# Issue order of every engine from a list schedule that the kernel makes over its own trace

## The chip, the cores and the metric

The kernel runs on one core of a Trainium2 chip. The core has five engines with instruction queues of their own: TensorE (PE, matmuls, with its weight loads as PEld), VectorE (DVE), ScalarE (ACT), GpSimd (POOL) and SyncE (SP, which only issues transfers). The metric is the device time of one execution in microseconds. The kernel before took 3448.2 us (median of three executions, 3447.78 to 3453.78).

## The reference

A decoder of four layers in float32, on x of 8 batches x 256 tokens x 256 features, with a context of 8 x 77 tokens. Every sublayer is followed by a residual and a layer normalisation:

```python
x = _layernorm(x + _L0_attn_ref(x, ...), axis=-1)           # causal, 16 heads, 8-bit fake quantisation
x = _layernorm(x + _L0_xattn_ref(x, ctx_1024, ...), axis=-1)  # 16 heads of 64
x = _layernorm(x + _L0_ffn_ref(x, ...), axis=-1)            # 8 experts, 2 per token, gelu
x = _layernorm(x + _L1_attn_ref(x, ...), axis=-1)           # causal softmax attention
x = _layernorm(x + _L1_xattn_ref(x, ctx_1024, ctx_1024, mask, ...), axis=-1)
x = _layernorm(x + _L1_ffn_ref(x, ...), axis=-1)            # 8 experts with a capacity, and a shared one, silu
x = _layernorm(x + _L2_attn_ref(x, ...), axis=-1)           # linear attention, elu features
x = _layernorm(x + _L2_xattn_ref(x, ctx_1024, ...), axis=-1)  # normalised heads, rope on q
x = _layernorm(x + _L2_ffn_ref(x, ...), axis=-1)            # 14 experts, 2 per token, and 2 shared ones
x = _layernorm(x + _L3_attn_ref(x, ...), axis=-1)           # state space layer: conv, chunked scan
x = _layernorm(x + _L3_xattn_ref(x, ctx_1024, ...), axis=-1)  # linear attention
x = _layernorm(x + _L3_ffn_ref(x, ...), axis=-1)            # butterfly up, exact gelu, butterfly down
```

The quantisation of layer 0 scales by maxima over all tokens, so it needs every batch before it can go on. The routed feed-forwards need the routing of all tokens before the first expert tile.

## The kernel before, in words

The class `Build` holds the program. Tokens lie in 16 tiles `x` of 128 x 256 and, transposed, in four tiles `xt`. The attention sublayers loop over the 8 batches of 256 tokens; each batch goes through a few hand-offs from PE to DVE, ACT and POOL and back. Helpers spread the work: `later` and `tick` keep generators of unfinished work, and a loop takes a step of them where the author placed a call, so that the end of one batch is traced between pieces of the next. `side` and `fill` do the same for weights and shared experts. The source's order is therefore already interleaved by hand.

All matmuls go through `mm` (line 164), which writes a PSUM tile of 512 float32 columns from `ps()`. These tiles share one tag, `ps`, in a pool of eight buffers, one for each bank. Most other tiles have a tag with one to five buffers.

The routed feed-forwards (`routed_tiles`, lines 1121 to 1133) run a fixed number of tiles (`U0`, `U2` = 19, 22), then a conditional block for more. POOL fetches each tile's weights and rows by indirect transfers (lines 1068 and 1093), DVE copies the result out (line 1166) and SP stores it. The next sublayer collects the results: `collected` gathers rows on POOL (line 1093) and adds them on DVE (line 2796), once per tile and choice.

The program's order on each engine is not written out. A scheduler of the language takes the traced instructions and decides the issue order of every engine and the buffer of every tile, in keeping with data dependencies. Where its order was not wanted, the author tied instructions with `after` (line 1039): the adds of line 2796 wait for the previous add and for marks set in the running loop (`gate`, `gates`, `mark`); the weight maximum of line 352 waits for the input maximum of line 477; the copy of line 1864 waits for the routing of the batch before (`routed`); the butterfly weights of lines 2505 and 2524 wait for the last expert tile (`tile_end`).

In layer 3, one loop over batches does the state space layer, the cross-attention and the feed-forward. Its activations use several function tables: silu (L2176), exp (L2211, L2433), exact gelu (L2361), for instance:

```python
for n in range(2):
    nc.scalar.activation(E[n], E[n], AF.Exp, scale=-1.0)
```

## Time and profile before

The profiled execution took 3453.26 us, of which the span from first to last instruction is 3451.5 us, with a mean granted clock of 0.908. By stages, in microseconds (PE and DVE are busy times; the clock is the granted share of TensorE's full clock):

| Stage from:to | Length | PE | DVE | Clock | What runs |
|---|---|---|---|---|---|
| 0:86.3 | 86.3 | 41.08 | 63.26 | 0.68 | loads, quantisation of layer 0 |
| 86.3:431.4 | 345.1 | 256.29 | 264.11 | 0.73 | layer 0 attention |
| 431.4:517.7 | 86.3 | 67.23 | 46.48 | 0.79 | its projection, cross-attention begins |
| 517.7:776.6 | 258.9 | 245.15 | 156.37 | 0.95 | layer 0 cross-attention, routing |
| 776.6:1035.4 | 258.8 | 258.80 | 28.09 | 1.00 | layer 0 experts |
| 1035.4:1121.7 | 86.3 | 76.20 | 43.13 | 0.88 | collecting, layer 1 attention begins |
| 1121.7:1294.3 | 172.6 | 170.79 | 108.58 | 1.00 | layer 1 attention |
| 1294.3:1380.6 | 86.3 | 73.88 | 53.64 | 0.92 | layer 1 cross-attention begins |
| 1380.6:1553.2 | 172.6 | 164.33 | 139.79 | 1.00 | layer 1 cross-attention |
| 1553.2:1639.5 | 86.3 | 76.72 | 44.86 | 0.80 | routing |
| 1639.5:2157.2 | 517.7 | 513.38 | 108.18 | 1.00 | layer 1 experts |
| 2157.2:2416.0 | 258.8 | 226.54 | 169.04 | 0.97 | layer 2 attention |
| 2416.0:2674.9 | 258.9 | 206.79 | 166.79 | 0.77 | layer 2 cross-attention |
| 2674.9:2847.5 | 172.6 | 172.02 | 74.08 | 1.00 | layer 2 experts |
| 2847.5:2933.8 | 86.3 | 78.57 | 33.51 | 0.93 | collecting |
| 2933.8:3365.2 | 431.4 | 367.72 | 301.78 | 0.89 | layer 3 |
| 3365.2:3451.5 | 86.3 | 63.24 | 26.65 | 0.90 | last batches of layer 3 |

An engine that waits for nothing in a stage bounds it. PE's busy time counts a matmul until its modelled end, so a high share is not yet full work; [...]busy time times clock says how much full-clock work was done.

### The profile page before, as it was taken

The page shows a single profiled execution, that of the slowest core. Times are in us where ns is not written, and L with a number is a line of the kernel's source. Part 1 is how long each engine was busy: PE and PEld are TensorE (multiplying, and loading weights), DVE is VectorE, ACT ScalarE, POOL GpSimd, SP SyncE. Part 2 cuts the span into 40 slices and gives each one's busy share as a digit, 9 for nine tenths or more (in the row PEclk, how much of TensorE's full clock was granted, in tenths as well). Part 3 has the DMA queues.
Part 4 walks back from the last instruction along what each step waited for, and adds up shares of the span by engine and source line. Part 5 has one row for each costly group of instructions (what it writes and reads, how often), then busy time and mean ns, then how long its engine had stood idle before and what let it go on. Part 6 is the DMA issues. An engine that isn't in the chain of part 4 may idle for free. (4 is left out here: it accounts for less than half of the span.)

```text
span 3451.5 us, 49595 instructions
## 1 busy us (share of the span) xinstructions
PE 3058.7 (89%) x19199; PEld 2186.5 (63%) x19210; DVE 1828.4 (53%) x4835; ACT 1082.8 (31%) x2426; POOL 932.6 (27%) x1379
## 2 busy tenths in 40 slices
PE   4787679989998998998999999998787999888887
PEld 3444357768886776665555777565555786567766
DVE  7887556641005666785111221576675443687763
ACT  4666422222222333332111111344222112244332
POOL 2222323343312211232000000331333563433331
PEclk6777779989998999998999999999787999889998
DMA  9900110025532000001010343100002562000000
GB/s 337 333 1 2 37 44 13 19 82 197 183 134 86 19 30 14 20 14 59 14 37 12 117 139 114 42 20 8 7 20 68 193 216 90 25 7 4 7 7 10
DMA packets 132658, 239.96 MB, mean 70 GB/s; under 512 B 14585, under 2 KB 104449, under 8 KB 124737
## 3 DMA queue, kind: packets, MB, share of 16 engines
q1 hardware_dynamic: 108160, 136.71, 11.9%
q0 software_dynamic: 23104, 98.95, 8.4%
q8 instruction: 156, 2.56, 0.3%
q10 hardware_dynamic: 1152, 1.05, 0.1%
q14 instruction: 86, 0.70, 0.1%
HBM read 156.98 MB, written 79.69 MB: 69 GB/s over the span
## 5 line engine op out<-in xcount | busy, mean ns | idle before, releaser
L164 PE MATMUL ps<-xt,w 128*128 128x256 f32 (+1 forms) x1408 | 446.4, 466 | 8.7 <-issue 8.7
L164 PE MATMUL ps<-w,hT 128*128 128x256 f32 (+1 forms) x1792 | 397.4, 379 | 0.0
L164 PEld LDWEIGHTS ps<-w,hT 128*128 128x128 f32 (+1 forms) x1792 | 329.9, 186 | 56.5 <-issue 6.0
L164 PE MATMUL ps<-gT,w 128*128 128x256 f32 (+1 forms) x1472 | 356.9, 400 | 5.7 <-ACT gT L152 3.0
L164 PEld LDWEIGHTS ps<-xt,w 128*128 128x128 f32 x1408 | 264.8, 195 | 151.2 <-issue 129.8
L164 PEld LDWEIGHTS ps<-gT,w 128*128 128x128 f32 x1472 | 276.2, 191 | 76.6 <-ACT gT L152 3.9
L164 PE MATMUL ps<-w,oT 128*128 128x256 f32 x704 | 165.0, 390 | 1.1 <-ACT oT L152 0.2
L164 PEld LDWEIGHTS ps<-w,oT 128*128 128x128 f32 x704 | 135.6, 195 | 34.0 <-issue 11.1
L1155 ACT ACTIVATE hT<-ps,more 128x256 f32<-128x256 f32 x152 | 72.0, 474 | 199.0 <-PE ps L164 199.0
L1166 DVE COPY y<-ps 128x512 f32<-128x512 f32 x41 | 28.3, 690 | 174.8 <-PE ps L164 174.8
L1232 DVE TENSOR_TENSOR hT<-hT,ps 128x512 f32<-128x512 f32 x56 | 38.5, 688 | 149.9 <-PE ps L164 149.5
L694 ACT ACTIVATE e<-ps,nm 128x128 bf16<-128x128 f32 (+1 forms) x256 | 103.9, 458 | 39.9 <-DVE nm L689 23.9
L244 PE MATMUL ps<-ident,x 128*128 128x128 f32 x288 | 57.3, 311 | 61.8 <-DVE x L272 46.9
L272 DVE TENSOR_SCALAR x<-res,mv,rs 128x256 f32<-128x256 f32 x112 | 51.4, 459 | 111.6 <-POOL rs L192 111.6
L284 POOL TENSOR_TENSOR xb<-x,rows 128x256 f32<-128x256 f32 x80 | 61.4, 773 | 178.0 <-DVE res L289 174.1
L1228 ACT ACTIVATE hT<-ps 128x512 f32<-128x512 f32 x56 | 33.4, 597 | 237.7 <-PE ps L164 237.7
L1723 POOL TENSOR_TENSOR kpad<-kpad,rows 128x256 f32<-128x256 f32 (+1 forms) x10 | 7.3, 730 | 363.5 <-DVE hu L1672 276.2
L911 POOL TENSOR_TENSOR P<-P,z 128x1232 f32<-128x1232 f32 (+1 forms) x32 | 55.2, 1736 | 169.6 <-DVE z L910 169.6
L978 PE MATMUL ps<-PT,V 77*64 77x256 f32 x512 | 95.0, 429 | 6.6 <-ACT PT L152 4.4
L1587 ACT ACTIVATE f<-ps,neg 128x512 f32<-128x512 f32 x128 | 77.4, 689 | 57.2 <-PE ps L1584 57.2
L963 PEld LDWEIGHTS ps<-ident,P 128*77 128x77 f32 x512 | 60.1, 155 | 51.7 <-issue 23.9
L1588 DVE SCALAR_TENSOR_TENSOR f<-ps,f 128x512 f32<-128x512 f32 x128 | 79.0, 680 | 25.8 <-ACT f L1587 25.8
(670 smaller groups left out, 6436.1 us busy)
## 6 DMA issues: line engine op xcount, KB each, us to landing
l2x<-zero SPq DMA_DIRECT2D x28, 1024.0 KB, 11.2
l0x<-zero SPq DMA_DIRECT2D x16, 1024.0 KB, 10.8
w<-in_L_ffn_rg SPq DMA_DIRECT2D x8, 1024.0 KB, 7.0
w<-in_L_ffn_ru SPq DMA_DIRECT2D x8, 1024.0 KB, 5.0
w<-in_L_ffn_rd SPq DMA_DIRECT2D x8, 1024.0 KB, 5.6
l2e<-y SPq DMA_DIRECT2D x22, 256.0 KB, 2.3
l0e<-y SPq DMA_DIRECT2D x19, 256.0 KB, 2.5
w<-in_L_xattn_Wk SPq DMA_DIRECT2D x4, 1024.0 KB, 5.0
```

Of the source, the lines that this page charges most:

```text
L164: self.nc.tensor.matmul(out, lhsT, rhs, start=(i == 0), stop=(i == last))
L244: self.nc.tensor.transpose(ps[:, k * P : (k + 1) * P], x[:, k * P : (k + 1) * P], self.ident)
L272: nc.vector.tensor_scalar(t, r, mv[:, 0:1], rs, ALU.subtract, ALU.mult)
L284: self.nc.gpsimd.tensor_tensor(t, self.X[i], row, ALU.add)
L694: nc.scalar.activation(e[:, : (t + 1) * P], ps[j][:, i, :], AF.Exp, bias=nm[:, t, h : h + 1], accum_out=z[:, t, h : h + 1],)
L911: eng.tensor_tensor(pr, pr, z.unsqueeze(2).to_broadcast([P, n, SC]), ALU.mult)
L963: nc.tensor.transpose(psv[:, m, t * P : (t + 1) * P], Pt[t][:, 2 * n + m, :], self.ident)
L978: nc.tensor.matmul(po[64 * m : 64 * m + 64, :S], V[:, h * 64 : (h + 1) * 64], ahead[n % 2][:, m, :], start=True, stop=True,)
L1155: nc.scalar.activation(hT[:, f + m, :], ps[:, m * 256 : (m + 1) * 256], func, bias=more[:, f + m : f + m + 1])
L1232: nc.vector.tensor_tensor(hT[:, f, :], hT[:, f, :], ps, ALU.mult)
L1587: nc.scalar.activation(f[:, j], ps[j], AF.Exp, bias=neg1)
L1588: self.mark = nc.vector.scalar_tensor_tensor(f[:, j], ps[j], 1.0, f[:, j], ALU.max, ALU.min)
```

## The change

The kernel is now traced twice. The first trace ends in a new class `Arrange`, which reads the traced instructions, works out their dependencies and durations, and makes a list schedule: for each engine it looks at up to 30 ready instructions not more than 300 places past the oldest unfinished one, and takes the first in source order that can start within `SLACK` of the earliest. It places PSUM tiles in banks as it goes. The second trace puts each PSUM tile under the tag of its bank, and ties every instruction to the one before it on its engine, so that the language's scheduler has no choice left. The ties that the author had made by hand are taken out; those that guard rows in memory (`scattered`, `zeroed`) stay.

```diff
+class Arrange:
+    ENGINES = ("PE", "DVE", "Activation", "Pool", "SP")
+    SIGNAL = {("DVE", "Pool"): 77, ("Activation", "Pool"): 69, ("PE", "Pool"): 100, ("DVE", "PE"): 44, ("Activation", "PE"): 43, ("Pool", "Pool"): 77}
+    TABLES = [{f, "Identity", "Copy", "Square", "Relu", "Abs"} for f in ("Exp", "Ln", "Silu", "Gelu", "Gelu_apprx_tanh")]
+    WINDOW, LOOK, RESERVE, SPAN = 300, 30, 2, 3413.0
+    SLACK = {"PE": 100, "DVE": 150, "Activation": 200, "Pool": 200, "SP": 0}
...
+    def cost(self, nd):
...
+        if kind == "InstMatmult":
...
+            own = n / 2.4 * (1 if not wide or turn else 4) + 3
...
+        if kind == "InstDMACopy":
...
+            return (1250 if e == "Pool" else 60), 1900 + nbytes / 210
...
+        if e == "DVE":
...
+            s = 65 + n / 0.96
...
+            return s, s + 95
+        if e == "Activation":
...
+            s = 144 + 0.83 * n + (108 if last else 0) + (45 if not ps and 64 < n <= 512 else 0)
+            return s, s + (40 if 500 < n < 600 else 105)
+        if kind == "InstTensorTensor":
+            s = 360 + 190 * n if n <= 8 else 145 + 2.13 * n
...
+        def place(nd):
...
+                if g[0] == "ps":
+                    mine, front = self.first[t].at, self.first[queue[g][head[g]]].at
+                    held = any(f.done is None and f.at < mine for f, _ in self.fences)
+                    kept = sum(last[k] < front for _, k in free)
+                    free = [
+                        (at, k) for at, k in free
+                        if last[k] < mine and not (held and k < 2)
+                        and (mine == front or last[k] > front or kept > self.RESERVE)
+                    ]
...
+                elif queue[g][head[g]] != t:
+                    return None
...
+                    more = 0
+                    if nd.func and (table is None or nd.func not in table):
+                        more = 1294
+                    st = max(st + more, ready(nd), p[0])
...
+                    low = min(o[0] for o in opts) + self.SLACK[e]
+                    o = next(o for o in opts if o[0] <= low)
...
+                while window < st // self.SPAN:
+                    speed = 1.0 if filled > self.SPAN * (0.58 if speed == 1.0 else 0.9) else 0.5
...
+    def chain(self, ranks):
+        info = mybir.DependencyInfo(mybir.DependencyClass.NoSync, mybir.DependencyReason.DATA)
+        tie = lambda y, x: self.tc.add_manual_dep(y, x.name, info, reason="order")
+        for nds in ranks.values():
+            for x, y in zip(nds, nds[1:]):
+                tie(self.listed[y], self.listed[x])
...
     def t(self, pool, shape, tag, dt=F32, bufs=None):
         self.n += 1
-        return pool.tile(list(shape), dt, tag=tag, name=f"{tag}_{self.n}", **({} if bufs is None else {"bufs": bufs}))
+        key = tag
+        if self.plan is not None and pool is self.psp:
+            key, bufs = f"ps{self.plan[1].get(self.n, self.n % 2)}", 1
+        t = pool.tile(list(shape), dt, tag=key, name=f"{tag}_{self.n}", **({} if bufs is None else {"bufs": bufs}))
+        self.made[t.tensor.name] = pool.name, tag, bufs or pool.bufs, self.n
+        return t
...
-        ins = self.absmax(m, WT)
-        if behind is not None:
-            self.after(ins.ins, [behind.ins])
+        self.absmax(m, WT)
...
-                        ins = nc.vector.tensor_copy(o[:, 2 * gp : 2 * gp + 2, :], ps)
-                        if routed is not None:
-                            self.after(ins.ins, [routed.ins])
+                        nc.vector.tensor_copy(o[:, 2 * gp : 2 * gp + 2, :], ps)
...
-                if k == 1:
-                    self.after(op.ins, [self.tile_end.ins])
...
-                    add = nc.vector.scalar_tensor_tensor(g.X[i], y, self.wt[:, k, i : i + 1], g.X[i], ALU.mult, ALU.add)
-                    if g.gate is not None:
-                        g.after(add.ins, [g.gate.ins])
-                    if g.gates:
-                        g.after(add.ins, [g.gates.pop().ins])
-                    g.gate = add
+                    nc.vector.scalar_tensor_tensor(g.X[i], y, self.wt[:, k, i : i + 1], g.X[i], ALU.mult, ALU.add)
...
+        if plan is None:
+            raise Planned(Arrange(g).order())
+        Arrange(g).chain(plan[0])
```

## The prediction

> **What bounds the kernel now.** I read the page's head and slices first, for what is busiest and what clock TensorE (PE) is granted.
>
> ```profile
> PE 3058.7 (89%) x19199; PEld 2186.5 (63%) x19210; DVE 1828.4 (53%) x4835; ACT 1082.8 (31%) x2426; POOL 932.6 (27%) x1379
> ...
> PEclk6777779989998999998999999999787999889998
> ```
>
> PE is the busiest engine, but 89% is an average over stages, and a busy microsecond at a low clock is worth less than one at full clock. So next I cut the span into stages; columns are length, then busy time of PE, PEld, DVE, ACT, POOL, then granted clock, DMA share, GB/s.
>
> ```profile
> 86.30:431.40 345.10, 256.29 (x2829) 138.88 (x2830) 264.11 (x615) 211.22 (x689) 99.30 (x191) 0.73 0.28 93
> ...
> 1380.60:1553.20 172.60, 164.33 (x1090) 117.80 (x1088) 139.79 (x427) 66.93 (x151) 53.15 (x66) 1.00 0.05 17
> ...
> 1639.50:2157.20 517.70, 513.38 (x1855) 337.40 (x1854) 108.18 (x260) 70.18 (x148) 13.56 (x17) 1.00 0.21 72
> 2157.20:2416.00 258.80, 226.54 (x1956) 148.17 (x1965) 169.04 (x391) 108.00 (x189) 70.87 (x118) 0.97 0.08 23
> 2416.00:2674.90 258.90, 206.79 (x1636) 144.43 (x1637) 166.79 (x584) 65.35 (x154) 94.13 (x142) 0.77 0.09 32
> ...
> 2933.80:3365.20 431.40, 367.72 (x1893) 290.47 (x1893) 301.78 (x791) 168.16 (x264) 149.70 (x231) 0.89 0.03 10
> ```
>
> Busy time times clock is PE's work in full-clock microseconds. The stage from 1639.5 (layer 1's feed-forward) has 513 in 517.7: no order can shorten it. The stage from 86.3 (layer 0's attention) has 256.29 x 0.73 = 187 in 345.1: PE idles for 89 and loses 69 to the clock. Taking length minus busy x clock over all 17 stages of the table above gives, in order, 58, 158, 33, 26, 0, 19, 2, 18, 8, 25, 4, 39, 100, 1, 13, 104 and 29, together some 638 us. That is all that better order could ever win; 2813 us is the floor. No other engine fills a stage: DVE comes closest, with 81% in the stage from 1380.6, while PE there has 95% at full clock.
>
> Then the chain of waits that ended last, inside the last layer (start, length, engine, line; a piece of 1.28 with no tile is an activation-table load), and the group of those loads.
>
> ```profile
> 3277.47 1.28 ACT L2211
> 3278.77 1.48 ACT l2s L2211
> 3280.79 1.28 ACT L2361
> 3282.09 1.57 ACT hT L2361 x4
> 3283.67 1.28 ACT L2211
> 3284.97 1.49 ACT l2s L2211
> 3286.47 1.28 ACT L2361
> ```
> ```profile
> L2211 ACT ACT_TABLE_LOAD x12 | 15.4, 1283 | 0.2
> L2361 ACT ACT_TABLE_LOAD x12 | 15.4, 1283 | 0.2
> ```
>
> The source writes both L2211 activations next to each other; the engine runs them with L2361 between and reloads the table each time, on the path. So the order now in force is not the source's, and whoever made it did not price that load.
>
> [...]stage clocks lie between 0.68 and 1.00 and follow PE's load. [...]the activation starts 0.02 us after the load (3277.47 + 1.28 against 3278.77), so I price 1.28 and no drain.
>
> **The change, part by part.**
>
> *The order itself.* No arithmetic is added or removed: PE's 2813 full-clock us stay. What moves is the order in which the 49595 recorded instructions reach the head of their queues, among them the 264 DMA issues of SP and the 375 indirect ones of POOL. Whether the plan holds on the chip depends on its durations, so I compare them with rows. Its DVE formula gives a 128x512 reduction 65 + 512/0.96 + 95 = 693 ns, the trace has 682 (L716); ACT on 128x256 from PSUM 144 + 212 + 105 = 461, the trace 474 (L1155); POOL's power 360 + 190 + 50 = 600, the trace 555 (L192); POOL's cast 100 + 461 + 50 = 611, the trace 615 (L773); POOL on 128x1232 2819, the trace 2255 (L911, too dear by 25%); DVE on 128x256 in SBUF 427, the trace 500 (L2161, too cheap by 15%). A 1 MB load is 1.9 + 5.0 = 6.9 us, the trace 5.0 to 7.0; zero fills take 11.2, but nobody waits for those soon. [...]A plan this near should mostly hold.
>
> What it can win I take from this kernel: the stage from 1380.6 shows that PE at 95% or DVE at 81% is reachable with these eight PSUM banks. A stage's reachable length is the larger of PE work / 0.952 and DVE busy / 0.81. For the looped stages: 86.3, max(196, 326), saves 19; 517.7, max(245, 193), saves 14; 2157.2, max(231, 209), saves 28; 2416, max(167, 206), saves 53; 2933.8, max(344, 373), saves 59. Sum 173. For the stages between (0, 431.4, 1035.4, 1294.3, 1553.2, 2847.5, 3365.2) the same division gives 8 + 29 + 16 + 15 + 22 + 9 + 27 = 126, but those wait for a maximum over all tokens, for routing tables or for the first and last transfers, which order cannot shorten. The plan looks 300 source instructions ahead and picks greedily, and tiles in SBUF keep their order. I take 60% of 173 = 104, and 20% of 126 = 25. Bounds: from 0 to 299 won, and a loss is possible (rival below).
>
> *Table loads.* The plan prices a switch at 1294 ns, so L2211's pair and L2361's pair should stand together: 12 + 12 loads become about 8 + 8, 8 x 1.28 = 10 us less on ACT, on the path where the chain shows them. This is part of the 59, not added.
>
> *PSUM tiles tagged by bank.* No instruction; 0. The cover is that the eight banks stay in use; only tiles inside the two conditional blocks are confined to two. Those blocks did not run: 38 and 44 gathers of gx are 2 x 19 and 2 x 22, the unconditional tiles. Had they run, each would pay PE waits for evictions of 0.4 to 0.7 us.
>
> *Hand-made ties out.* They hold the 96 adds of gathered rows (L2796) back on DVE, with scattered others (weight maximum, L1865, L2510, L2526). Without them an add could head DVE's queue before its gather lands and hold up every eviction behind it, PE with them. The row of L2796 shows 19.3 us idle before it now. The plan schedules the landing 1.25 + 1.9 + 0.62 + 0.05 = 3.8 us after the issue; the trace has a median of 2.8, a longest of 6.6. So the plan itself covers it: 0, between -19 and, if all late gathers cost 3 us once per batch in three layers, 24 x 3 = +72.
>
> *Second trace.* Made while building; nothing runs on the chip.
>
> Sum against the profiled execution, 3453.3: -104 - 25 = -129, so 3324. The median of the runs shown is 3448.2, 5 lower; I predict **3320**.
>
> **Rivals.**
> *Stronger.* Denser PE also gets the clock back: the half-clock loss is busy minus busy x clock, 3058.7 - 2813 = 246 of the 638 us, most of it in stages 86.3 (69), 2416 (48) and 2933.8 (40). If all 173 and half of 126 come, 3448 - 236 = 3212. Against: DVE already binds at 81% in the yardstick.
> *Weaker.* The looped stages are tied by their chains (PE, DVE, POOL, DVE through each normalisation; DVE waits 111.6 us for POOL's L192), and only a fifth of 173 comes, plus the table loads: 3448 - 45 = 3403.
> *No effect.* The order the builder finds is already as good: within 0.2%. The split table loads speak against.
> *Slower.* PE, sent ahead by the plan, fills banks that DVE empties later than planned (L2161's 15%), stands still, and falls to half clock. [...]For it: clock in three stages is already 0.73 to 0.89, so little is needed.[...]
>
> **How the numbers follow.** Base 0.58 (3270 to 3375), stronger 0.15 (3200 to 3270), weaker 0.13 (3375 to 3441), no effect 0.04, slower 0.10. Measurement of this kernel tells 0.2%, 7 us. Faster is 0.58 + 0.15 + 0.13 = 0.86. The range 3200 to 3441 holds the first three, 0.86, with a little of the stronger case falling below it.
>
> **What would show it.** In the changed profile: mean clock over 0.93 and PE idle well below 392 us; the stages of layer 2's cross-attention and of layer 3 shorter by some 30 us each or more; the feed-forward stages unchanged; table loads fewer than 70, L2211 and L2361 near 8 each; idle before L2796 not above 20 us. It would be wrong if the clock fell, PE waited on DVE or ACT evictions, or DVE waited for gathers.

## The result, and the profile after

The changed kernel takes 3396.01 us (median of four, 3387.93 to 3401.54) against 3448.98 for the kernel before on the same chip: a ratio of 0.9842, 95% interval 0.9818 to 0.9866. The forecast was 3320, a gain of 129 us; the gain is 53. The profiled execution took 3401.54, its span 3399.8 us.

First the page of the kernel after: the engines' busy times, then the granted clock and the DMA share in 40 slices of 85 us.

```profile
PE 3104.2 (91%) x19192; PEld 2225.2 (65%) x19210; DVE 1927.5 (57%) x4835; ACT 1079.2 (32%) x2420; POOL 925.3 (27%) x1379
...
PEclk6667679999997999999999999999877899999998
...
DMA  9000010006579200001101033310000365200000
```

And the DMA slices of the kernel before.

```profile
DMA  9900110025532000001010343100002562000000
```

TensorE (PE) stands still less: span less busy is 3399.8 - 3104.2 = 296 us, before 3451.5 - 3058.7 = 393. But its busy time grew by 45 us with the same matmuls at nearly the same mean clock (0.914, before 0.908). In every record of both traces (136 before, 100 after) the granted clock is either 1 or 0.5, and float32 matmuls of 128x256 back to back start every 216 ns at clock 1 and every 427 ns at 0.5. So PE's work in full-clock time can be summed stretch by stretch: busy time under clock 1 plus half of that under clock 0.5. It is 2825 us before and 2886 after. And a block of transfers has moved: before, the first two slices are full; after, the second is empty and the 12th and 13th (935 to 1105 us) are fuller.

To see where, I cut both spans at the same pieces of work (ends of the same instruction in both traces; microseconds):

| From - to | Before | After | Change |
|---|---|---|---|
| start - last output add of layer 0's attention | 401.8 | 446.0 | +44.2 |
| - layer 0's cross-attention begins | 81.4 | 67.7 | -13.7 |
| - layer 0's expert tile 11 copied out | 445.0 | 429.3 | -15.7 |
| - expert tile 19 copied out | 113.7 | 159.6 | +45.9 |
| - layer 1's attention begins | 39.9 | 34.9 | -5.0 |
| - last exponential of that attention | 219.6 | 235.7 | +16.1 |
| - layer 1's experts begin | 321.8 | 292.4 | -29.4 |
| - they end | 517.4 | 517.2 | -0.2 |
| - layer 2's cross-attention ends | 490.4 | 468.4 | -22.0 |
| - layer 2's experts end | 257.2 | 252.0 | -5.2 |
| - layer 3's first convolution | 96.1 | 79.5 | -16.6 |
| - its last one | 333.1 | 300.1 | -33.0 |
| - last residual add | 125.8 | 109.8 | -16.0 |

The steps that got shorter sum to 157 us, more than was forecast. Three got longer, by 106. The gain did not fail to come; it was given back in three places. Windows (length, then busy PE, PEld, DVE, ACT, POOL, clock, DMA share, GB/s) of the kernel after, in layer 0's attention, layer 2's cross-attention and layer 3:

```profile
85.00:446.00 361.00, 301.02 (x2768) 160.80 (x2768) 252.85 (x561) 200.10 (x657) 88.68 (x173) 0.68 0.01 4
...
2483.00:2651.00 168.00, 158.70 (x1306) 117.24 (x1310) 126.14 (x422) 54.66 (x125) 64.55 (x90) 0.78 0.05 18
...
2983.00:3393.00 410.00, 368.91 (x2011) 298.83 (x2009) 318.10 (x767) 159.77 (x268) 144.50 (x226) 0.95 0.02 8
```

The same pieces of work in the kernel before:

```profile
85.00:402.00 317.00, 243.31 (x2779) 130.24 (x2778) 247.49 (x570) 201.05 (x668) 86.10 (x170) 0.74 0.29 97
...
2448.00:2631.00 183.00, 151.76 (x1360) 106.92 (x1352) 122.94 (x439) 53.06 (x127) 66.80 (x91) 0.80 0.05 18
...
2984.00:3443.00 459.00, 386.22 (x1998) 312.44 (x1996) 298.65 (x763) 170.94 (x277) 141.54 (x223) 0.89 0.02 7
```

Layer 3 is the forecast come true: less time, a clock of 0.95 instead of 0.89. Layer 0's attention is the opposite: PE does the same matmuls in 301 us instead of 243, at a lower clock. With records of either 1 or 0.5, a mean of 0.68 over 361 us is 231 us at half clock, and 0.74 over 317 is 165.

The chain of waits that ended last, in layer 3 of the kernel after (start, length, what):

```profile
3241.57 1.52 PE ps L2630 x16
3243.09 1.07 PE ps L559 x4
3244.23 1.28 ACT L2749
3245.53 0.84 ACT hT L2749 x2
3246.37 1.05 ACT zs L2642 x2
```

One table load (the 1.28 with no tile) before two gelus (L2749 was line 2361), and then squares, which start at 3246.37, the gelus' end, with no load between, where the chain of before had four loads within 9 us. The largest groups of loads:

```profile
L2821 ACT ACT_TABLE_LOAD x10 | 12.8, 1283 | 4.7 <-DVE kv L2820 4.5
L2749 ACT ACT_TABLE_LOAD x9 | 11.5, 1283 | 6.0 <-PE ps L559 5.9
```

In all there are 64 loads instead of 70; from layer 3's first convolution on there are 26 instead of 36.

### The profile page after: what moved, and what is told of

The parts are those of the page before. It is cut to its first block, busy times and chain, and to the rows that moved or that the text cites. A ratio compares the mean times of both kernels' runs of the same rounds, so it can differ in the third digit from the quotient of the medians.

```text
span 3399.8 us, 49404 instructions
## 1 busy us (share of the span) xinstructions
PE 3104.2 (91%) x19192; PEld 2225.2 (65%) x19210; DVE 1927.5 (57%) x4835; ACT 1079.2 (32%) x2420; POOL 925.3 (27%) x1379
## 5 line engine op out<-in xcount | busy, mean ns | idle before, releaser
L559 PEld LDWEIGHTS ps<-xt,w 128*128 128x128 f32 x1408 | 257.7, 190 | 153.5 <-issue 121.5
L1300 ACT ACTIVATE P<-P 128x616 f32<-128x616 f32 (+1 forms) x48 | 42.6, 888 | 161.3 <-DVE P L1341 161.3
L1356 PE MATMUL ps<-ident,P 128*77 128x128 f32 x512 | 82.4, 290 | 10.8 <-DVE P L1304 6.4
L1109 DVE TENSOR_REDUCE cm<-ps 128x2 f32<-128x512 f32 (+1 forms) x96 | 60.1, 683 | 53.4 <-PE ps L1050 53.4
L1016 PE MATMUL ps<-kd,qT 32*128 32x128 bf16 (+1 forms) x512 | 66.7, 289 | 23.4 <-ACT e L1087 14.2
```

The costliest lines, as they stand in the source:

```text
L559: self.nc.tensor.matmul(out, lhsT, rhs, start=(i == 0), stop=(i == last))
L1016: nc.tensor.matmul(ps[j][:, i, :], v["q"][r, g, t * P : (t + 1) * P], v["k"][r, g // 2, :n], start=(i == 0), stop=False)
L1109: nc.vector.tensor_reduce(cm[:, at : at + len(gs)], ps[j], AX.X, ALU.max)
L1300: nc.scalar.activation(pr, pr, AF.Exp, scale=0.125)
L1356: nc.tensor.transpose(psv[:, m, t * P : (t + 1) * P], Pt[t][:, 2 * n + m, :], self.ident)
```

## The experiments

The kernel before takes 3449 to 3451 us on two of the chips used and 3487 to 3491 on the others, and the changed kernel's ratio is 0.9842 on the first kind and 0.9794 on the second (one chip each). So each kernel below has its ratio to the kernel before on its own chip, and ratios are compared on chips of the same kind; where that isn't possible, the text says so. "First kind" and "second kind" mean these two.

### Where the zero fills went

Layer 2's table of rows is set to zero by 28 transfers of 1 MB on SP's queue. The kernel before starts them at 74 to 154 us, the changed one at 986 to 1081, among layer 0's expert tiles. In the source they stand at layer 1's attention, and the plan lets no engine look more than 300 places past the oldest unfinished instruction. The theory before these runs was that there they take the bandwidth from the experts' weights.

*sp_free* takes that limit off SP alone:

```diff
-                while heap and len(look) < self.LOOK and heap[0][0] <= nodes[oldest].at + self.WINDOW:
+                while heap and len(look) < self.LOOK and (e == "SP" or heap[0][0] <= nodes[oldest].at + self.WINDOW):
```

> The plan may take SP's transfers from any distance ahead; all else is planned as in the changed kernel. Theory (the 28 zero fills of l2x, 1 MB each, now issued from 986 us, crowd out the weight fetches of layer 0's last experts): the fills move back before 100 us, the step from expert tile 11 to 19 goes from 160 us to about 114, and the time falls by 35 to 45 us, to 3351 to 3361. Rival (the experts' end is late because of the order around the conditional block): the fills move and the time stays within 8 us of 3396.

Measured: ratio 0.9696 (0.9673 to 0.9718), second kind, which is 0.0098 or some 34 us below the changed kernel there; the fills start at 74 to 154 us again, and expert tiles 11 to 19 take 113.7 us, as before the change.

*before_late_fill* is the reverse, on the kernel before: the same fills are asked for at expert tile 14.

```diff
...
+                if j == 14:
+                    self.slot_rows(2, self.tile_end)
...
-            self.slot_rows(2)
```

> The kernel before with one thing moved: layer 2's zero fills (28 transfers of 1 MB) are asked for at expert tile 14 of layer 0 and wait for its end, about where the changed kernel issues them; all else is the kernel before. Theory 'fills against weights': the step from expert tile 11 to 19 grows from 113.7 us to 145-165, as in the changed kernel, the whole by 25-45 us: ratio 1.007 to 1.013. Rival 'order inside the experts' (the plan's own order of the expert tiles is what stretched them): the step stays at 113-118 us and the ratio within 0.002 of 1.

Measured: ratio 1.0120 (1.0103 to 1.0137), first kind; the step takes 158.1 us instead of 113.7. Windows from tile 11 to tile 19; kernel before:

```profile
928.00:1042.00 114.00, 113.17 (x538) 97.44 (x536) 10.55 (x16) 30.35 (x64) 20.50 (x22) 1.00 0.38 137
```

After, with waits of PE and VectorE (DVE) in that window (total, times, longest):

```profile
943.00:1103.00 160.00, 119.55 (x552) 102.07 (x551) 10.71 (x18) 30.35 (x64) 20.38 (x22) 0.88 0.86 296
...
DVE y L1561 <- DMA l0e<-y: 78.2, 3, 51.8
...
PE ps L559 <- DVE gT L1511: 32.7, 1, 32.7
```

before_late_fill:

```profile
928.00:1087.00 159.00, 113.52 (x540) 97.73 (x538) 10.89 (x16) 30.36 (x64) 20.76 (x22) 0.87 0.82 281
```

sp_free:

```profile
950.00:1064.00 114.00, 114.00 (x542) 98.27 (x541) 10.62 (x16) 30.35 (x64) 20.56 (x22) 1.00 0.39 137
```

PE is busy 113 to 120 us in all four. With the fills there, the transfers move 281 to 296 GB/s instead of 137, and PE stands still for 40 us or more. Taken away, the loss goes; put into the other kernel, it comes. That the fills cause it is shown: 44 to 46 us of the step, 1.2% of the whole when put in, 1.0% when taken out.

The way in which they do it is not the theory's. The weight fetches, which GpSimd (POOL) issues, land 8.4 and 9.3 us after their issue (medians of the two weights from 985 us on) instead of 7.0 and 5.6, and no wait for them shows in this step. What waits are the results. The experts' results are stored by SP too, and a store is issued only after the fills that stand ahead of it there (start, length, what; kernel after):

```profile
1014.39 49.82 SPq L1420 DMA_DIRECT2D l2x<-zero  x15
1064.31 2.92 SPq L1562 DMA_DIRECT2D l0e<-y  x1
```

The issue of one fill holds SP for 3.0 us (median of the 28), where a store in the kernel before holds it for 0.36. A result that was ready at 1000.1 us is therefore stored from 1064.3 on. There are two buffers `y`, so the copy of the third result waits 51.8 us for that store (the line of DVE above), and the copy of the next tile's turned rows `gT`, which PE waits for, stands behind it in DVE's queue: PE had turned those rows by 1035.3 us, and the two copies run at 1073.5 and 1074.1. before_late_fill has the same wait, and PE loses its time there in one wait of 45.6 us for DVE's queue at the end of the step:

```profile
DVE y L1168 <- DMA l0e<-y: 63.7, 1, 63.7
```

In the kernel before and in sp_free no copy of `y` waits for a store. The plan could not see this: its constants let SP issue a transfer in 60 ns and eight transfers run side by side. Fills left in place with the stores on another engine's queue would have tested it directly; that was not run.

### Row-tiled matmuls that no longer overlap

In the attentions, the source gives matmuls of 32 rows each one of four row positions (row groups, below) and goes round them in fours. In the traces such neighbours run at once: in the first group below, 120 matmuls of 529 ns each keep PE busy for 19.1 us. *l0_pe_source* keeps PE in source order inside layer 0's attention (all else planned), and *sp_free_l0_pe* does that together with sp_free:

```diff
...
+            if nd.e == "PE" and at < self.stop:
+                if self.before_pe is not None:
+                    nd.preds.add(self.before_pe)
+                self.before_pe = nd
...
```

> Within layer 0's attention PE keeps the source's order; the other engines and all later stages are planned. Theory (PE's reordering breaks up groups of four 32-row matmuls and keeps the clock at half): PE changes line some 490 times instead of 729 in that stage, half-clock time falls from 236 us to about 166, the last L786 result comes at about 402 to 412 us instead of 446, and the time falls by 30 to 45 us, to 3351 to 3366. Rival (the order of DVE and ACT, or banks taken out of turn, cost the 44 us): the stage still ends after 435 us and the time stays within 10 us of 3396.

> Both edits. If both theories hold the savings add: 3396 - 41 - 40, 3310 to 3330. If only the fills matter, 3350 to 3362; if only PE's order, the same range by the other cause; if neither, 3390 to 3402.

Measured, second kind: l0_pe_source 0.9747 (0.9730 to 0.9765), its layer 0 attention ends at 428.3 us instead of 446.0 (before 401.8); both together 0.9627 (0.9609 to 0.9644). The attention's end lies between what the theory (402 to 412) and its rival (after 435) expected: PE's order gives back 18 of the 44 us. The two repairs add up: against the changed kernel's 0.9794 on such chips (after_again, below) 0.0098 and 0.0047 alone, 0.0167 together.

The groups of instructions by shape show what PE's order does: busy is the time in which at least one of the group runs, then the mean of one. The largest group of 32-row matmuls over 512 columns in layer 0's attention, in the kernel before:

```profile
L642 PE MATMUL ps<-qT,kd 32*128 32x512 bf16 x120 | 19.1, 529 | 0.6
```

After:

```profile
L1035 PE MATMUL ps<-qT,kd 32*128 32x512 bf16 x120 | 40.0, 536 | 2.0 <-ACT e L1161 0.8 <-DVE rm L1136 0.7 <-DVE cm L1109 0.3
```

With PE in source order (l0_pe_source):

```profile
L1040 PE MATMUL ps<-qT,kd 32*128 32x512 bf16 x120 | 20.7, 530 | 1.4 <-ACT e L1166 0.2
```

As many matmuls, each as long, and twice the time: 120 x 529 ns in 19.1 us is an overlap of 3.3, in 40.0 us 1.6. Summed from start to start over the 32-row matmuls (idle left out), layer 0's attention has 101 us of PE before, 147 after, 89 in l0_pe_source. So l0_pe_source has more than all of the overlap back, and its attention still ends 26 us later than before: lost overlap is not the whole loss there.

*quartets* starts from sp_free and keeps every run of row-tiled matmuls in source order, begun only when all its PSUM banks are free; *res4* is its control.

```diff
...
-    WINDOW, LOOK, RESERVE, SPAN = 300, 30, 2, 3413.0
+    WINDOW, LOOK, RESERVE, SPAN = 300, 30, 4, 3413.0
...
+                if max(p.pe[3]) < max(nd.pe[3]) or max(nd.pe[3]) == 0 and max(p.pe[3]) == 96:
+                    nd.preds.add(p)
+                    nd.run = p.run
+                    nd.run.append(nd)
...
+                if len(free) < need:
                     return None
```

(res4 is sp_free with the first of these edits alone.)

> The plan as in sp_free (its window not applied to SP), and in it every run of 32-row matmuls kept in source order and begun only when PSUM banks for all four row groups are free; so that this can't lock up, four banks instead of two are kept back for the oldest tiles. Theory 'split fours' (the plan issues row-tiled matmuls in twos as banks come free, and on the chip two cost the time of four): groups of four come back from about 78 to about 250 in layer 0's attention, TensorE's time on row-tiled matmuls falls there from 147 us to 85-105, in layer 1's attention from about 83 to about 62, in layer 2's cross attention from about 64 to about 45; layer 1's attention step gets 12-22 us shorter than in sp_free, the whole 30-75 us faster: ratio 0.948 to 0.961 against sp_free's 0.9696. Rival 'order at large' (the loss in the attentions comes from which stage's work is let in, not from the splitting): the ratio stays within 0.004 of that of res4, though the fours come back.

> sp_free with four instead of two PSUM banks kept back for the oldest tiles and nothing else: the control for quartets. Both theories: the twos stay (about as many split groups as in sp_free), the ratio lies within 0.006 of sp_free's 0.9696. If it moves as far as quartets does, the reserve and not the grouping is what works there.

Measured, first kind: quartets 0.9730 (0.9714 to 0.9746), res4 0.9724 (0.9708 to 0.9741). Layer 1's attention takes 214.9 us in quartets, 230.0 in res4, 235.7 in the changed kernel, 219.6 before. So where PE is the bound (busy for 222 of the 230 us in res4), the grouping gives 15 us back, as expected. But layer 0's attention ends at 454.2, no earlier than res4's 450.0. Its 32-row matmuls take 120 us instead of the 85 to 105 expected, and PE now waits 39 us for ScalarE there, 14 in the changed kernel. The whole is no faster: of the 18 us by which quartets leads at the end of layer 1's attention, half is gone at the end of the profiled run, all in the medians. The forecast of 0.948 to 0.961 was missed, and by the whole time the rival's line was met.

*before_pairs* and *before_singles* put the cause into the kernel before, in layer 1's attention: row groups 0 and 1 first and then 2 and 3, or one row group after the other.

```diff
...
-                        for i, g in enumerate(gs):
-                            for j, r in enumerate(rows):
+                        for j, r in enumerate(rows):
+                            for i, g in enumerate(gs):
...
```

(before_singles, at one of its two places; before_pairs goes over `two in ((0, 1), (2, 3))` outside and `j in two` inside.)

> The kernel before with one thing changed: in layer 1's attention the row-tiled score matmuls of most groups are written in twos of row groups (0, 1) and then (2, 3) instead of in fours; same matmuls, same count. Theory 'split fours': TensorE's time on row-tiled matmuls there grows from 59.5 us to 80-100, the step from layer 1 attention's first to last exponential from 219.6 us to 240-258, the whole by 18-38 us: ratio 1.005 to 1.011. Rival 'twos cost nothing' (as the plan's own price has it): step within 4 us, ratio within 0.002 of 1.

> The kernel before with one thing changed: in layer 1's attention the score matmuls are written row group by row group (both or all four of a row group's matmuls one after another, then the next row group) instead of going round the four row groups; same matmuls, same count. Theory 'neighbours on one row group cannot overlap': TensorE's time on row-tiled matmuls there grows from 59.5 us to 80-115, the step from layer 1 attention's first to last exponential from 219.6 us to 235-265, ratio 1.004 to 1.013. Rival 'the way in which row groups follow one another costs nothing': step within 4 us, ratio within 0.002 of 1.

Measured: before_pairs 0.9996 (0.9987 to 1.0005), step 220.5 us; before_singles 1.0039 (1.0025 to 1.0053), step 250.5, part of that the chip's (a clock of 0.97 in it instead of 0.99). One group of layer 1's scores; kernel before:

```profile
L1353 PE MATMUL ps<-q,kT 32*128 32x128 f32 x256 | 13.0, 291 | 0.0
```

After:

```profile
L1748 PE MATMUL ps<-q,kT 32*128 32x128 f32 x256 | 20.3, 284 | 0.0
```

quartets:

```profile
L1757 PE MATMUL ps<-q,kT 32*128 32x128 f32 x256 | 9.4, 283 | 0.0
```

before_pairs:

```profile
L1357 PE MATMUL ps<-q,kT 32*128 32x128 f32 x256 | 13.8, 283 | 0.0
```

before_singles:

```profile
L1353 PE MATMUL ps<-q,kT 32*128 32x128 f32 x256 | 24.9, 285 | 0.3
```

By their ratios, twos look free: before_pairs is where its rival put it. The start times in the traces say otherwise. In a whole four of this group the starts are 7 ns apart, and the next four starts 112 ns after the first. In before_pairs a two starts every 112 ns, in before_singles mostly one or two every 105 to 112 ns. Counted by starts within 40 ns of the one before, this group is made up so:

| Kernel | Busy us | In fours | In twos | Alone |
|---|---|---|---|---|
| quartets | 9.4 | 100% | 0 | 0 |
| before | 13.0 | 78% | 11% | 11% |
| before_pairs | 13.8 | 38% | 62% | 0 |
| after | 20.3 | 2% | 66% | 29% |
| before_singles | 24.9 | 0 | 48% | 52% |

So twos do cost, for each matmul some twice the time of fours (112 ns for two against 112 for four), and the group of the kernel before was itself not whole. before_pairs changed little because this was the only one of layer 1's four such groups that came out differently. One other was not edited, and two start as they did before, since the language's scheduler and not the source makes the issue order. It is no test of the theory of fours, which the table supports. In before_singles, too, only the two groups of 128 columns were broken up.

What costs is the time from one start to the next: in this group 112 ns for a four (before) and for a two (after), and 103 ns for a single one (after; medians), so that it hardly falls when fewer run at once. (In these groups each row group also writes a bank of its own, so the row group and the bank come back together; no run tells the two apart.) The four groups sum to 63 us before, 64 in before_pairs, 90 in before_singles and 89 in the changed kernel, 59 in quartets. The cost is shown from both sides in layer 1's attention, where 26 us of it lengthened the step by 16; put into the kernel before, it costs 0.4%, 14 us.

This is also where PE's added full-clock work lies: 2825 us before and 2886 after become 2827 in quartets, 2814 in mix and 2826 in l0_language (both below), where the fours are back, and before_singles has 2854.

The plan's own price invites the splitting. It looks at the matmul just before and no further (`own` is one matmul's time alone, `pos` and `pos2` the row groups of the two, `j` the number of the first):

```python
...
        if wide:
            half = max(own / 2 - 13, 96)
...
            return own if pos == pos2 else half if j % 2 else 13
...
        return own if pos == pos2 else 4 if j < 3 else max(own - 36, 20)
```

Back to row group 0 after row group 1 thus costs half a matmul in float32 (`wide`) and 4 ns in bfloat16, so that twos cost no more for each matmul than fours. Whether this price or the banks, which come free one at a time, split the groups was not tried apart.

### What else is lost in layer 0's attention

Four kernels start from quartets. *mix* adds PE's source order in layer 0's attention. *hold90* changes one constant of the plan's clock, so that it counts on full clock less often. *l0_untied* leaves layer 0's attention to the language's scheduler, with the plan's banks; *l0_language* gives it the eight rotating buffers back as well.

```diff
-                    speed = 1.0 if filled > self.SPAN * (0.58 if speed == 1.0 else 0.9) else 0.5
+                    speed = 1.0 if filled > self.SPAN * (0.9 if speed == 1.0 else 0.9) else 0.5
```

(hold90)

```diff
...
         for nds in ranks.values():
+            nds = [y for y in nds if y >= self.stop]
             for x, y in zip(nds, nds[1:]):
...
+                if plan is not None:
+                    g.ps_stack.close()
+                    g.psp = g.ps_stack.enter_context(tc.tile_pool(name="ps2", bufs=8, space=PSUM))
+                    g.free_l0 = False
...
```

(l0_language; l0_untied leaves out the ties into instructions before `stop` and changes no pool.)

> quartets (SP free of the window, runs of row-tiled matmuls kept together, four banks kept back) with TensorE also kept in source order inside layer 0's attention. If the two repairs add up: layer 0's attention ends at 425-435 us instead of 454, the ratio falls from 0.973 to 0.965-0.969. If layer 0's attention is lost to something that neither touches (the order of the other engines, or the banks), the ratio stays at 0.971-0.975.

> quartets with one constant of the plan's clock changed[...]. Theory 'the plan is too hopeful about the clock, so it packs TensorE's half-clock stages badly': layer 0's attention ends 8-30 us earlier than in quartets, layer 2's cross attention gets 3-15 us shorter, ratio 0.960-0.970. Rival 'the order hardly depends on the assumed clock': ratio 0.971-0.975, attention within 5 us of 454.

> quartets with the planned order not tied for the instructions of layer 0's attention: the language's scheduler orders them as in the kernel before, the planned PSUM banks stay, the rest of the kernel keeps the plan. Theory 'the plan's order is what costs in layer 0': its attention ends at 395-415 us instead of 454, the ratio falls to 0.957-0.964. Rival 'the banks cost': with PSUM tiles bound to banks the language's order is no better, the attention ends after 435 us, ratio 0.970 or more.

> quartets, but layer 0's attention left wholly to the language's scheduler: no planned ties there and its PSUM tiles in the eight rotating buffers of the kernel before (the PSUM pool is closed at the attention's end and a new one opened, in which the plan's banks and order hold). Theory 'what costs in layer 0 is the planned order and the banks that were chosen for it': its attention ends at 398-410 us instead of 454 (quartets) or 423 (mix), the whole gains 10-25 us on mix: ratio 0.951-0.959 against mix's 0.960. Rival 'something before or beside it': the attention still ends after 420 us. A cost of the change of pools would show as a later start of layer 0's cross attention (over 70 us after the attention's end).

Measured, all second kind:

| Kernel | Ratio (95%) | Layer 0's attention ends | Cross-attention begins | 32-row matmuls in the attention, us | Of them in fours |
|---|---|---|---|---|---|
| mix | 0.9602 (0.9586 to 0.9618) | 423.4 | 490.1 | 87 | 85% |
| hold90 | 0.9717 (0.9701 to 0.9733) | 446.3 | 515.7 | 122 | 77% |
| l0_untied | 0.9849 (0.9821 to 0.9877) | 495.5 | 573.6 | 191 | 32% |
| l0_language | 0.9584 (0.9564 to 0.9603) | 405.8 | 487.2 | 101 | 79% |

For comparison, the kernel before has 401.8 us, 101 us and 78%, the changed kernel 446.0, 147 and 30%, quartets 454.2, 120 and 78%. quartets has no run on the second kind, so its whole time can't be set against these four.

mix repairs what quartets alone did not (423 against 454). hold90's attention ends 8 us earlier than quartets', at its theory's lower edge; its ratio is where the rival put it, and a gain in the whole is not shown. l0_untied is the surprise: the language's order in banks chosen for another order ends the attention later than either kernel does. The largest group again, l0_untied:

```profile
L1047 PE MATMUL ps<-qT,kd 32*128 32x512 bf16 x124 | 44.3, 525 | 3.8 <-DVE rm L1148 1.5 <-ACT e L1173 1.2 <-DVE cm L1121 0.7
```

l0_language, where order and buffers belong together again:

```profile
L1055 PE MATMUL ps<-qT,kd 32*128 32x512 bf16 x120 | 18.8, 529 | 0.6
```

So the whole loss in layer 0's attention came with the plan's order and its banks: without them it ends at 405.8, within 4 us of the kernel before. But the plan is better just behind it (67 us to the cross-attention in mix, 81 in l0_language), and in both runs expert tile 19 is copied out at 1048.1 us, so the two differ by no more than their intervals. Whether the 20 us between 423 and 402 lie in the plan's orders of the other engines or in its banks stays open. Whole fours alone don't suffice: quartets has as many of them as the kernel before, and its attention ends 52 us later.

### The price of function tables

```diff
-                        more = 1294
+                        more = 0
```

> The changed kernel as it is, as the yardstick on this chip: ratio 0.981 to 0.987, expert step from tile 11 to 19 at 155-163 us, layer 0's attention ending at 443-449 us.

> The changed kernel with one constant of its plan changed: the price of a change of ScalarE's function table is 0 instead of 1294 ns. Theory 'the price of tables is part of the gain in layer 3 and layer 0': table loads rise from 64 to 75-110, layer 3 or layer 0's attention gets 5-40 us longer, ratio 0.002 to 0.012 above after_again. Rival 'ScalarE has slack where the tables change': within 0.002 of after_again, whatever the count.

Measured, on one chip of the second kind: after_again 0.9794 (0.9770 to 0.9818), a little below what was expected; no_table_price 0.9895 (0.9862 to 0.9928), 29 us longer by the medians (3451.6 against 3422.3) and inside its theory's range. Windows of layer 3, after_again:

```profile
3011.00:3419.00 408.00, 365.76 (x2012) 296.78 (x2010) 316.56 (x765) 159.55 (x268) 142.37 (x225) 0.95 0.02 8
```

no_table_price:

```profile
3007.00:3445.00 438.00, 382.22 (x2015) 309.05 (x2013) 316.38 (x767) 182.17 (x285) 140.08 (x225) 0.93 0.02 7
```

ScalarE is busy 22.6 us longer, and its 17 added instructions are the 17 added table loads (43 against 26, each 1.28 us). First to last convolution takes 324.5 us instead of 297.4. So 27 us hang on this constant, but not all of them count towards the 33 gained: without the price the plan makes 43 loads, more than the 36 of the kernel before. In proportion, the 10 loads that the change saved are worth 27 x 10 / 17 = 16 us, an estimate.

### The ties taken out

*ties_out_only* has the change's source without ties and without a plan; the language's scheduler orders it. *gather_price* is l0_language with gathers that the plan expects 3 us later.

```diff
-        if plan is None:
-            raise Planned(Arrange(g).order())
-        Arrange(g).chain(plan[0])
```

(ties_out_only)

```diff
-            return (1250 if e == "Pool" else 60), 1900 + nbytes / 210
+            return (1250 if e == "Pool" else 60), (4900 if e == "Pool" else 1900) + nbytes / 210
```

(gather_price)

> The hand-made ties are out and the language's scheduler makes the order; no plan, PSUM tiles in one group of eight as before. If the ties were worth something under that scheduler, slower than before: up to 72 us if late gathers block DVE once per batch in three layers (3460 to 3520), idle time before L2796 above 20 us. If they were worth nothing: 3441 to 3456.

> l0_language with one constant of the plan changed: it takes POOL's transfers to land 3 us later than it did, so that it places what uses them, the adds of the gathered expert rows among them, further behind their gathers. Theory 'the adds stand at the head of VectorE's queue before their rows have landed, and that is on the path': idle before the adds falls from 39 us to under 25, the whole by 5-17 us, ratio 0.953 to 0.957 against l0_language's 0.9584. Rival 'the path there is the gather itself and nothing else is ready': idle before the adds may fall, the time doesn't, ratio within 0.002 of 0.9584 or above.

Measured, second kind: ties_out_only 1.0095 (1.0075 to 1.0115), gather_price 0.9576 (0.9551 to 0.9601). The adds of gathered rows (busy, mean, then idle of VectorE just before them), after:

```profile
L3180 DVE SCALAR_TENSOR_TENSOR x<-gy,rwt,x 128x256 f32<-128x256 f32 x96 | 46.9, 492 | 36.2 <-DMA gy<-l0e,rsrc 14.2 <-DMA gy<-l2e,rsrc 11.6 <-DMA gy<-l1e,rsrc 9.4
```

gather_price:

```profile
L3200 DVE SCALAR_TENSOR_TENSOR x<-gy,rwt,x 128x256 f32<-128x256 f32 x96 | 45.9, 482 | 16.4 <-DMA gy<-l0e,rsrc 7.9 <-DMA gy<-l2e,rsrc 7.5
```

The ties were worth 0.95% to the order they were made for; without them the idle time before the adds is 35.3 us in place of 19.3. Under the plan it is as long (36.2; l0_language 39.2), and a better price takes more than half of it away. But the ratio moves by 0.0008, inside both intervals, where the theory expected 0.0014 or more: the rival's line was met. That wait costs the planned kernel little or nothing that was measured.

gather_price, 3342.35 us where the kernel before takes 3487.01, has the lowest median of all; mix, l0_language and gather_price beat both kernels and are not told apart.

## Why the prediction was wrong

A gain of 129 us was forecast and 53 came: the order gained more than that, and three losses, which the prediction had put at nothing or counted as a gain, took 106 us back.

- *Right:* the kernel is faster, by a time inside the range, and nearly every stage without one of the three losses got shorter. With the fills and the two attentions repaired the ratio is 0.9584 to 0.9602 (second kind), and the forecast's was 3320 / 3448 = 0.963.
- *Partly luck:* the gains add up to 157 us where 129 were forecast, but not where they were forecast. The looped stages of layer 0's cross-attention and layers 2 and 3 gave 71 us (15.7 + 22.0 + 33.0, by the cuts above) of the 60% of 154 = 92 counted for them. The cuts that hold the stages between gave 81 (13.7 + 5.0 + 29.4 + 16.6 + 16.0), where the prediction took 25, saying that order could not shorten them; the 29.4 hold layer 1's cross-attention as well.
- *"PE's 2813 full-clock us stay" failed first.* They grew by 61 us (2825 to 2886, summed as above; the prediction's 2813 came from rounded means by stage). How long PE takes for row-tiled matmuls depends on their neighbours (layer 1's four groups: 63 us before, 89 after), so a new order changes the work itself. The yardstick (PE work / 0.952, DVE busy / 0.81) took that work as given, and the comparison of the plan's prices with the trace had rows for DVE, ACT, POOL and a load, and none for PE.
- *The saving of 19 us (60% of it counted) in the stage from 86.3* was a loss of 44 by the attention's end. The rival "slower" was right that PE would fall to half clock there (165 to 231 us), but not for its reason, a late VectorE: that has the same 250 us of work in both windows, while PE needs 301 us for what took 243. PE's order explains 18 to 22 of the 44 us (l0_pe_source, mix), the plan's other orders and its banks the rest (l0_language), by a way that stays open.
- *"Zero fills take 11.2, but nobody waits for those soon"* was the second failure. Nobody does wait for the fills, but the experts' results stand behind them in SP's queue, and that cost 44 to 46 us. SP's 264 issues were counted among what moves and then given no cost, and the prediction's own worry about DVE, that an add waiting for its rows holds up what stands behind it, was not carried over to SP. The stage of layer 0's experts, which runs at full clock without a gap, was taken as one that order does not change.
- *Layer 1's attention* was in no sum, as a stage full at clock 1.00; it lost 16 us to the first failure.
- *Table loads:* the mechanism was right and the term small: 10 us were forecast as part of the 59 in layer 3, and the estimate above is 16. L2211 has 2 loads left and L2361 has 9, where some 8 each were forecast; L2433 went from 7 to 10.
- *PSUM tags at 0* holds only together with the order they were planned for: under another order in layer 0 the attention ended at 495 us instead of 454.
- *Ties at 0* was right in time under the plan, as far as gather_price shows, though the sign that it named (idle before the adds not above 20 us) came out at 36.
- *The rival "weaker"* gave 3403, near the measured time, but by another way: the looped stages of layers 2 and 3 did gain, 22 and 33 us. The nearness is luck: gains of 157 us less losses of 106 that no sum had.
- *Of the signs:* PE idle fell well below 392 (296), table loads fell below 70, layer 1's feed-forward stayed; the clock stayed at 0.914, not above 0.93, and layer 2's cross-attention gained 15 us from first to last exponential, not 30. Of the signs of being wrong, the clock fell in layer 0's attention (0.74 to 0.68), and VectorE waited longer for gathers.

## What to carry to other kernels

When a schedule is replaced, list not only what it makes denser but what the old order did without being asked: transfers that ran where nothing urgent stood behind them, and matmuls whose neighbours let them overlap; look up the busy time of the same shape in both traces, because the same count and mean with twice the busy time (here 120 of 529 and 536 ns, 19.1 and 40.0 us) is lost overlap. Ask of every bulk transfer what stands behind it in its queue: nobody waited for the fills, but results and, through two buffers, PE (32.7 us in one piece) waited for what they held up. A price for a matmul that looks at one neighbour is not enough where four run at once, their starts 7 ns apart. Buffers chosen for one order should not be kept under another. And an experiment that changes the source has to be checked in the trace: the order that was asked for may not be the order that ran.

## What the runs showed of the hardware

- The granted clock of TensorE is 1 or 0.5 in every record of the traces of both kernels (136 before, 100 after). Back to back, float32 matmuls of 128x256 (L164 of the kernel before) start every 216 ns at clock 1 and every 427 ns at 0.5, while the recorded length of one goes from 379 to 634 ns only.
- SP, which starts transfers, was itself held up. While the kernel after issued 28 fills of 1 MB, the issue of one took 3.0 us of SP's time (median; 0.6 to 6.8), where a store of 256 KB takes 0.36 us otherwise, and a store behind them was issued 64 us after its data was ready. PE stood still for 32.7 us in one piece, and the clock over the 160 us of that window was 0.88, against 1.00 over the same tiles in the kernel before. Weight fetches on POOL's queue in the same time landed only 1 to 4 us later.
- Float32 matmuls of 32 rows by 128 columns: 256 records took 9.4 us at best (quartets) and 24.9 at worst (before_singles), by their order on the row groups and the banks that go with it; the mean of one was 283 to 291 ns. From start to start a four took 112 ns (before), a two 112 and a single one 103 (after; medians).
- Chips differ more than some changes do: the same kernel took 3449 and 3490 us, and the same change gave 0.9842 and 0.9794. In layer 1's attention the changed kernel had clock 1.00 on the one and 0.97 on the other.
